# A selective state-space stage on Trainium2: two spare columns per scan row, the norm's root as a power on GpSimd, the residual added by TensorE, 14 instead of 12 products on GpSimd, and another order of all steps

## The chip, the cores and the metric

The kernel runs on one core of one Trainium2 chip. The metric is the time of one execution in microseconds of the device. Engines are named as in the profile: PE (TensorE), DVE (VectorE), ACT (ScalarE), POOL (GpSimd) and SP, whose queue only issues DMAs. Each engine works off its own queue in order, and engines wait for one another by semaphores.

## What is computed

The whole program is a small network over an image of 2 x 256 x 56 x 56: window attention, then six Mamba layers, then two token networks. The change touches only the six Mamba layers, a stage on tokens of width 256 with an inner width of 512 and 16 states per channel. For a batch row of 3136 tokens each layer computes:

```
residual = hidden + residual                  # width 256
x  = residual * rsqrt(mean(residual**2) + 1e-5) * norm_w
u, z = split(x @ in_w)                        # 512 each
u  = silu(causal_conv4(u) + cb)
dt_r, B, C = split(u @ xp_w)                  # 16, 16, 16
dt = softplus(dt_r @ dt_w + dt_b)
h_t = exp(dt_t * A) * h_(t-1) + (dt_t * u_t) * B_t    # 512 x 16 states
y_t = sum over states of h_t * C_t, plus u_t * D
hidden = (y * silu(z)) @ out_w
```

A layer norm stands in front of the first layer and one more root-mean-square norm behind the last.

## The kernel before

`mamba_phase` cuts the 3136 tokens into 7 chunks of T = 448. With 2 batch rows and 6 layers there are 84 chunks, worked through one after the other; a chunk index j runs over them. Inside a chunk the 512 x 16 states are taken in 32 **steps**, index s: 4 blocks k of 128 channels, 4 groups of states, 2 halves. One step handles two rows of T tokens on 128 partitions, side by side in one tile.

A step consists of these operations, each a small function:

- `inputs` (L809): ACT copies the state kept from the chunk before into the first column of each row of the tile `x`, and POOL multiplies `dtur` (dt times u, spread over partitions) by B (`bc`) into the other columns (L816).
- `decays` (L791): ACT computes exp(dt * A) into the PSUM tile `da`, one instruction for each of the two rows (L799). Column 0 of `dtr` holds 1e30, so that the decay there is 0 and the scan starts afresh in each row.
- `scan` (L833): one DVE instruction runs the recurrence over both rows, 2 x 449 = 898 columns. Its result goes back into `da`, or into `x` where the step is listed in `on_pool`.
- the product with C (`times_c`, L829): on DVE directly behind the scan, or, for the 12 steps of `on_pool`, later on POOL in place in `x` (`pool_product`).
- `keep` (L823): ACT copies the last column of each row into the state.
- `gather` (L840), for every second step: PE sums over states into the PSUM tile `acc`; `gate` (L857), for every eighth: DVE multiplies by silu(z).
- `fetch`: SP loads `dtr` and `dtur` for the next k from DRAM.

Beside these 32 steps the projections for the next chunk run: `u_project`, `u_convolve`, `x_project`, `dt_project` and others on PE, all through a single PSUM bank `mm`, each followed by a copy or an activation on ACT. `y_project` (L696) multiplies by `out_w`, and `y_add` (L705) adds the result to the residual on DVE. The norm takes `n_squares` (ACT square, PE mean), `n_root` (ACT, Sqrt), `n_invert` (DVE, reciprocal), `n_spread` (PE) and `n_weighted` (DVE). The tables `first` and `last` hold the same for the layer norm in front and the final norm. Tiles `x` come from a pool of 9 buffers, `da` from 3, `acc` and `mm` from one each.

The order is written out by hand: every operation gets a **place** in units of steps, a number added to the index of its step or chunk, and all are issued sorted by place. A place is thus no time; it only fixes the order of each engine's queue. Before, all steps have the same offsets:

```
put(i - 1.652, inputs, i)
put(i - 1.217, decays, i)
put(i + 0.4, scan, i)
put(i + 1.080, keep, i)
if i % ns in on_pool: put(i + 2.886, pool_product, i)
if i % 2 == 1: put(i + 3.900, gather, i)
if i % 8 == 7: put(i + 4.422, gate, i)
```

Of the kernel before, what the change touches and what calls it, by code (L numbers as in the profile page):

```python
# [453 lines left out]
def mamba_phase(ctx: ExitStack, tc: tile.TileContext, I, t1_d, t2_d):  # L454
# [9 lines left out]
    ctx.enter_context(tc.manual_schedule())  # L464
    T = MT
    cp = ctx.enter_context(tc.tile_pool(name="mb_const", bufs=1))
# [12 lines left out]
    nc.vector.memset(mean_w, 1.0 / C)  # L479
    eps = ones_column(nc, cp, 1e-5, "mb_eps")  # L480
    sum_w = cp.tile([P, HD], F32, name="sum_w")
    nc.sync.dma_start(sum_w, I["sum_w"])
# [4 lines left out]
    res = cp.tile([P, 2, S], F32, name="res")  # L487
    dtrs = [cp.tile([P, 4, T + 1], F32, name=f"dtr{n}") for n in range(2)]
    for t in dtrs:
        nc.gpsimd.memset(t[:, :, 0:1], BIG)  # L490

    r1_d = [dp.tile([P, 2, T], F32, name=f"r1_d{c}", bufs=1) for c in range(MCH)]

    def wide(t, n=2):
        return t.unsqueeze(1).to_broadcast([P, n, T])

# [112 lines left out]
    def x_keep(j):  # L609

        xd = M["xd"] = one.tile([DTR + 2 * DS, T], F32, name="xd")
        nc.scalar.copy(xd, M["mm"])  # L612
        bc_d = dp.tile([2 * DS, T], F32, name="bc_d")
        nc.sync.dma_start(bc_d, xd[DTR:, :])
        bc = QS[j + 1]["bc"] = two.tile([P, 8, T + 4], F32, name="bc")[:, :, 3 : T + 3]
        for n in range(4):
            nc.sync.dma_start(
                bc[chunk(n, HD)],
                bc_d.rearrange("(m n) t -> n m t", n=4)[n].unsqueeze(0).to_broadcast([HD, 8, T]),
            )  # L620
        QS[j + 1]["dt_d"], QS[j + 1]["dtu_d"] = {}, {}
# [41 lines left out]
    def root(key):  # L663
        rs = M[key] = one.tile([MTG, ng], F32, name="rs" + key)
        nc.scalar.activation(rs, M["mm"][:MTG, :ng], AF.Sqrt, bias=eps[:MTG])

    def invert(key):
        nc.vector.reciprocal(M[key], M[key])

# [26 lines left out]
    def y_project(j, k):  # L696

        ps = M["mm"] = mm()[:, :T]
        for d in range(NB):
            nc.tensor.matmul(  # L700
                ps, lhsT=layer_of(j - 1)["w_out"][:, d, chunk(k, P)],
                rhs=QS[j - 1]["hz"][:, d, :], start=(d == 0), stop=(d == NB - 1),
            )

    def y_add(j, k):  # L705
        rc = residual(j - 1)
        nc.vector.tensor_tensor(rc[:, k, :], rc[:, k, :], M["mm"], ALU.add)  # L707

# [58 lines left out]
    def repeat(Q, k):  # L767

        dtr = dtrs[k % 2]
        dtur = two.tile([P, 4, T + 4], F32, name="dtur")[:, :, 1 : T + 1]  # L770
        for t, src in ((dtr[:, :, 1:], Q["dt_d"]), (dtur, Q["dtu_d"])):
            for n in range(4):
                nc.sync.dma_start(t[chunk(n, HD)], src[k].rearrange("(g p) t -> p g t", p=HD))
        Q[k] = dtr, dtur
# [4 lines left out]

    on_pool = (2, 3, 5, 7, 8, 9, 10, 15, 19, 21, 22, 26)  # L780
    chunks = [(b, layer, c) for b in range(B) for layer in range(NL) for c in range(MCH)]
# [9 lines left out]
    def decays(i):  # L791
# [3 lines left out]
        da = pda.tile([P, 1024], F32, name="da")  # L795
        D[i] = da[:, : 2 * (T + 1)]
        for g in range(2):
            col = (4 * k + 2 * pr + g) * 4 + ng
            nc.scalar.activation(  # L799
                D[i][:, chunk(g, T + 1)], dtr[:, 2 * pr + g, :], AF.Exp,  # L800
                scale=L["am"][:, col : col + 1],
            )
# [6 lines left out]
    def inputs(i):  # L809

        j, s, k, ng, pr = at(i)
        Q = QS[j]
        X[i] = xp.tile([P, 2 * (T + 1)], F32, name="x")
        x = both(X[i])
# [8 lines left out]
    def keep(i):  # L823
        h = X[i] if i % ns in on_pool else D[i]
        nc.scalar.copy(states(i), both(h)[:, :, T : T + 1])  # L825

    def times_c(i, engine, h):
        j, s, k, ng, pr = at(i)
        engine.tensor_tensor(  # L829
            both(X[i])[:, :, 1:], both(h)[:, :, 1:], wide(QS[j]["bc"][:, 4 + ng, :]), ALU.mult  # L830
        )

    def scan(i):  # L833

        h = X[i] if i % ns in on_pool else D[i]
        nc.vector.tensor_tensor_scan(h, D[i], X[i], 0.0, ALU.mult, ALU.add)  # L836
        if i % ns not in on_pool:
            times_c(i, nc.vector, h)

    def gather(i):  # L840
# [9 lines left out]
        for g in range(4):  # L850
            nc.tensor.matmul(  # L851
                acc[0][chunk(g, HD), :T], lhsT=sum_w, rhs=both(X[i - 1 + g // 2])[:, g % 2, 1:],
                start=False, stop=(ng == 3), tile_position=(0, HD * g),
# [8 lines left out]

    def pool_product(i):
        times_c(i, nc.gpsimd, X[i])

# [17 lines left out]
    def load_rest(j):  # L883
# [5 lines left out]
    places = {  # L889
        (u_project, 0): 1.304, (u_keep, 0): 2.607, (z_project, 0): 3.501, (z_keep, 0): 3.952,  # L890
        (u_project, 1): 4.609, (u_keep, 1): 5.234, (y_project, 1): 6.869, (y_add, 1): 7.331,
        (y_project, 0): 7.461, (y_add, 0): 9.223, (u_convolve, 0): 10.048, (u_add, 0): 10.687,
        (u_project, 2): 10.964, (u_keep, 2): 11.995, (u_convolve, 1): 12.277, (u_add, 1): 13.134,
        (u_convolve, 2): 14.792, (u_add, 2): 15.184, (u_project, 3): 15.393, (u_keep, 3): 16.616,
        (u_convolve, 3): 17.440, (u_add, 3): 17.991, (z_project, 1): 18.040, (u_silu,): 18.479,
        (z_keep, 1): 18.732, (x_project,): 19.334, (x_keep,): 20.167, (dt_project, 2): 20.825,
        (dt_keep, 2): 21.601, (dt_project, 0): 21.808, (dt_keep, 0): 22.204,
        (dt_project, 1): 23.295, (dt_keep, 1): 23.374, (dt_project, 3): 24.269,
        (dt_keep, 3): 24.913, (dt_softplus,): 24.942, (dt_out, 0): 25.013, (dt_back,): 25.337,
        (z_project, 2): 25.840, (dt_out, 1): 26.057, (z_keep, 2): 26.747, (z_project, 3): 27.262,  # L900
        (load,): 27.272, (dt_out, 2): 27.694, (z_keep, 3): 28.791, (n_squares,): 29.547,
        (n_root,): 29.821, (n_invert,): 31.105, (n_spread,): 32.629, (n_weighted,): 32.761,
        (load_rest,): 34.587, (dt_out, 3): 36.194, (z_silu,): 38.909,
    }
    first = {
        f_load: 12.141, f_mean: 23.145, f_center: 23.266, f_squares: 23.712, s_root: 23.835,
        s_invert: 24.267, s_spread: 25.138, f_scale: 25.476,
    }
    last = {
        l_squares: 0.000, s_root: 0.000, s_invert: 1.571, s_spread: 2.712, l_weighted: 3.271,  # L910
        f_load: 5.288, l_out: 5.690,
    }
# [14 lines left out]
    for i in range(n):  # L927
        put(i - 1.652, inputs, i)
        put(i - 1.217, decays, i)
        put(i + 0.4, scan, i)  # L930
        put(i + 1.080, keep, i)
        if i % ns in on_pool:
            put(i + 2.886, pool_product, i)
        if i % 2 == 1:
            put(i + 3.900, gather, i)
        if i % 8 == 7:
            put(i + 4.422, gate, i)
        if i % 8 == 0 and i % ns < ns - 8:
            put(i + 1.264, fetch, i)
    for j in range(-2, nj + 1):  # L940
# [559 lines left out]
```

## Time and profile before

| | before |
|---|---|
| median of 3 runs | 9829.77 us (9820.45 to 9840.27) |
| profiled execution | 9833.15 us, span 9831.3 us, granted clock 0.867 |
| first and last scan start | 693.4 us and 8489.3 us |
| DVE busy in the span | 8388.8 us (85%) |
| POOL busy | 7120.1 us (72%) |
| ACT busy | 6758.1 us (69%) |
| PE busy | 7995.7 us (81%) |

The profile is one execution. Its page gives busy time and counts of each engine, the span in 40 slices, the chain that ended last, and groups of instructions by line with their mean duration and the idle time before them. Durations of neighbours on one engine overlap a little; the time that an instruction takes from its engine is read from the starts of consecutive instructions in the timeline.

### The profile page before, as it was taken

How to read it: one execution, taken by the hardware profiler on the slowest of the kernel's cores; microseconds unless marked ns; L12 is line 12 of the kernel's file. 1: busy time of each engine (PE TensorE's matmuls, PEld its weight loads, DVE VectorE, ACT ScalarE, POOL GpSimd, SP SyncE). 2: the span in 40 equal slices, each digit the busy share in tenths (PEclk: the TensorE clock that was granted, in tenths of full speed). 3: DMA queues.
4: the chain of work that ended last, by engine and by line, in shares of the span. 5: the costliest groups of instructions: out<-in, count | busy, mean ns of one | idle time of the engine just before them, and what ended most of it. 6: DMA issues, size and time to landing. Idle time of an engine off the chain costs nothing. (4 is left out here: it accounts for less than half of the span.)

```text
span 9831.3 us, 102094 instructions
## 1 busy us (share of the span) xinstructions
PE 7995.7 (81%) x31026; PEld 3378.5 (34%) x31026; DVE 8388.8 (85%) x6835; ACT 6758.1 (69%) x15177; POOL 7120.1 (72%) x4860
## 2 busy tenths in 40 slices
PE   9877777777777777777777877787777777699999
PEld 6533323322222222232222222222222223255555
DVE  3338999899999999999999999999999999685453
ACT  1127777777877878777778787787877877534443
POOL 2347888788888888888898888888889888511110
PEclk9988888788888888888888888888888888799999
DMA  2235555455555555556555555555555555301111
GB/s 81 70 100 113 115 132 120 114 132 123 128 121 128 131 114 131 127 124 142 122 127 131 122 124 128 126 121 124 133 118 123 134 121 127 104 19 34 42 41 38
DMA packets 681950, 1083.41 MB, mean 110 GB/s; under 512 B 83532, under 2 KB 673169, under 8 KB 681169
## 3 DMA queue, kind: packets, MB, share of 16 engines
q1 hardware_dynamic: 681398, 1076.90, 47.1%
q8 instruction: 243, 3.98, 0.2%
q14 instruction: 309, 2.53, 0.1%
HBM read 891.71 MB, written 184.91 MB: 110 GB/s over the span
## 5 line engine op out<-in xcount | busy, mean ns | idle before, releaser
L816 POOL TENSOR_TENSOR x<-dtur,bc 128x896 f32<-128x896 f32 x2688 | 4706.5, 1775 | 109.6 <-PE acc L851 100.0
L799 ACT ACTIVATE da<-dtr,am 128x449 f32<-128x449 f32 x5376 | 3428.5, 638 | 188.1 <-DVE x L836 95.8
L836 DVE TENSOR_TENSOR_SCAN da<-da,x 128x898 f32<-128x898 f32 x1680 | 3397.1, 2022 | 144.7 <-ACT da L799 71.3
L829 POOL TENSOR_TENSOR x<-x,bc 128x896 f32<-128x896 f32 x1008 | 1791.2, 1777 | 510.6 <-ACT state L825 509.2
L554 PE MATMUL mm<-xn,w_in 128*128 128x448 f32 x2656 | 1483.3, 691 | 710.5 <-ACT hz L595 236.1
L836 DVE TENSOR_TENSOR_SCAN x<-da,x 128x898 f32<-128x898 f32 x1008 | 2001.8, 2013 | 0.7 <-ACT da L799 0.7
L829 DVE TENSOR_TENSOR x<-da,bc 128x896 f32<-128x896 f32 x1680 | 1834.4, 1092 | 80.6 <-PE mm L572 0.9
L851 PE MATMUL acc<-x,sum_w 128*32 128x448 f32 x10752 | 1565.9, 658 | 25.2 <-POOL x L829 17.7
L572 PE MATMUL mm<-u,w_cv 128*128 128x448 f32 x2656 | 1088.5, 552 | 175.5 <-ACT u L566 158.8
L554 PEld LDWEIGHTS mm<-xn,w_in 128*128 128x128 f32 x2656 | 550.3, 230 | 1684.5 <-issue 731.5
L825 ACT COPY state<-da 128x2 f32<-128x2 f32 x1680 | 264.2, 157 | 1059.4 <-DVE x L829 1041.8
L572 PEld LDWEIGHTS mm<-u,w_cv 128*128 128x128 f32 x2656 | 476.7, 189 | 801.5 <-issue 371.8
L644 POOL TENSOR_TENSOR dtu<-dt,hz 128x448 f32<-128x448 f32 x336 | 329.7, 981 | 463.4 <-ACT state L825 413.0
L700 PE MATMUL mm<-hz,w_out 128*128 128x448 f32 x1344 | 552.0, 554 | 80.2 <-DVE res L707 47.8
L625 PE MATMUL mm<-xd,w_dt 16*128 16x448 f32 x664 | 454.4, 772 | 190.7 <-ACT xd L612 111.1
L851 PEld LDWEIGHTS acc<-x,sum_w 128*32 128x32 f32 x10752 | 229.7, 117 | 1002.7 <-issue 792.2
L815 ACT COPY x<-state 128x2 f32<-128x2 f32 x2688 | 521.7, 194 | 0.0
L1348 DVE TENSOR_TENSOR hid<-hid,cb 128x784 f32<-128x784 f32 x128 | 135.2, 1057 | 423.8 <-ACT hid L1345 400.4
L799 ACT ACT_TABLE_LOAD x346 | 443.9, 1283 | 7.0 <-DMA dtr<-dt_d 1.0
L658 PE MATMUL mm<-mb_mean_w,sq 128*112 128x1 f32 x1744 | 259.5, 279 | 231.0 <-ACT sq L654 230.2
L846 PE MATMUL acc<-hz,w_sk 128*128 128x448 f32 x672 | 369.4, 635 | 63.1 <-DVE hz L861 61.8
L700 PEld LDWEIGHTS mm<-hz,w_out 128*128 128x128 f32 x1344 | 242.5, 190 | 403.7 <-issue 191.2
(217 smaller groups left out, 8949.1 us busy)
## 6 DMA issues: line engine op xcount, KB each, us to landing
dtr<-dt_d SPq DMA_DIRECT2D x1344, 224.0 KB
dtur<-dtu_d SPq DMA_DIRECT2D x1344, 224.0 KB
bc<-bc_d SPq DMA_DIRECT2D x336, 448.0 KB
dt_d<-dt SPq DMA_DIRECT2D x336, 224.0 KB
dtu_d<-dtu SPq DMA_DIRECT2D x336, 224.0 KB
cb<-comb_d SPq DMA_DIRECT2D x128, 196.0 KB
t<-t_d SPq DMA_DIRECT2D x28, 448.0 KB
w_in<-in_in_w SPq DMA_DIRECT2D x12, 1024.0 KB
```

What stands on the lines that cost most here:

```text
L554: nc.tensor.matmul(ps, lhsT=layer_of(j + 1)["w_in"][:, k, chunk(at, P)], rhs=Q["xn"][:, k, :], start=(k == 0), stop=(k == 1),)
L572: nc.tensor.matmul(ps, lhsT=layer_of(j + 1)["w_cv"][:, 4 * d + k, :], rhs=M["u", d][:, k : k + T], start=(k == 0), stop=(k == 3),)
L625: nc.tensor.matmul(ps, lhsT=layer_of(j + 1)["w_dt"][:, chunk(d, P)], rhs=M["xd"][:DTR, :], start=True, stop=True,)
L644: nc.gpsimd.tensor_tensor(dtu, dt[:, d, :], hz(j)[:, d, :], ALU.mult)
L700: nc.tensor.matmul(ps, lhsT=layer_of(j - 1)["w_out"][:, d, chunk(k, P)], rhs=QS[j - 1]["hz"][:, d, :], start=(d == 0), stop=(d == NB - 1),)
L799: nc.scalar.activation(D[i][:, chunk(g, T + 1)], dtr[:, 2 * pr + g, :], AF.Exp, scale=L["am"][:, col : col + 1],)
L815: nc.scalar.copy(x[:, :, 0:1], states(i))
L816: nc.gpsimd.tensor_tensor(x[:, :, 1:], Q[k][1][:, 2 * pr : 2 * pr + 2, :], wide(Q["bc"][:, ng, :]), ALU.mult)
L829: engine.tensor_tensor(both(X[i])[:, :, 1:], both(h)[:, :, 1:], wide(QS[j]["bc"][:, 4 + ng, :]), ALU.mult)
L836: nc.vector.tensor_tensor_scan(h, D[i], X[i], 0.0, ALU.mult, ALU.add)
L846: nc.tensor.matmul(acc[0][:, :T], lhsT=L["w_sk"][:, k, :], rhs=Q["hz"][:, k, :], start=True, stop=False,)
L851: nc.tensor.matmul(acc[0][chunk(g, HD), :T], lhsT=sum_w, rhs=both(X[i - 1 + g // 2])[:, g % 2, 1:], start=False, stop=(ng == 3), tile_posi ...
```

## The change

- Rows get two trailing columns: R = T + 3 = 451, a scan has 902 columns. `dtr`, `dtur` and `bc` hold zeros there (set once; `dtur` and `bc` become two fixed tiles each), so the decay is 1, the input 0, and the last column repeats the last state. `keep` reads the last column; the product with C covers only the T real ones. `inputs` on POOL is 2 x 450 wide.
- `root` uses ACT's Identity (adds 1e-5) instead of Sqrt; `invert` raises to the power -0.5 on POOL instead of a reciprocal on DVE.
- `y_project` gets a fifth matmul, identity times residual, in the same PSUM group; `y_keep` on ACT copies the sum into the residual instead of DVE's addition.
- `on_pool` lists 14 other steps. The product is an operation with a place of its own, on DVE too.
- `inputs`, `decays`, `product`, `keep`, `gather` and `gate` have places of their own for each step, and all places of the projections and norms are new.

```diff
+    half = ones_column(nc, cp, -0.5, "half")
...
-    dtrs = [cp.tile([P, 4, T + 1], F32, name=f"dtr{n}") for n in range(2)]
+    dtrs = [cp.tile([P, 4, R], F32, name=f"dtr{n}") for n in range(2)]
+    dturs = [cp.tile([P, 4, T + 4], F32, name=f"dtur{n}")[:, :, 1:R] for n in range(2)]
+    bcs = [cp.tile([P, 8, T + 4], F32, name=f"bc{n}")[:, :, 2:] for n in range(2)]
...
-        nc.scalar.activation(rs, M["mm"][:MTG, :ng], AF.Sqrt, bias=eps[:MTG])
+        nc.scalar.activation(rs, M["mm"][:MTG, :ng], AF.Identity, bias=eps[:MTG])
...
-        nc.vector.reciprocal(M[key], M[key])
+        nc.gpsimd.tensor_tensor(
+            M[key], M[key], half[:MTG].to_broadcast([MTG, ng]), ALU.pow
+        )
...
+        nc.tensor.matmul(ps, lhsT=ident, rhs=residual(j - 1)[:, k, :], start=False, stop=True)
...
-        nc.vector.tensor_tensor(rc[:, k, :], rc[:, k, :], M["mm"], ALU.add)
+    def y_keep(j, k):
+        nc.scalar.copy(residual(j - 1)[:, k, :], M["mm"])
...
-    on_pool = (2, 3, 5, 7, 8, 9, 10, 15, 19, 21, 22, 26)
+    on_pool = (0, 1, 4, 10, 11, 13, 14, 16, 19, 21, 26, 27, 28, 29)
...
-        nc.scalar.copy(states(i), both(h)[:, :, T : T + 1])
+        nc.scalar.copy(states(i), both(h)[:, :, R - 1 :])
...
+    def product(i):
+        if i % ns in on_pool:
+            times_c(i, nc.gpsimd, X[i])
+        else:
+            times_c(i, nc.vector, D[i])
...
+        (y_project, 1): 1.94872, (y_keep, 1): 2.18416, (y_project, 0): 4.51846,
+        (y_keep, 0): 4.93098, (u_convolve, 0): 5.73491, (u_add, 0): 6.45942,
...
+        (z_keep, 3): 25.37533, (n_squares,): 25.49637, (dt_out, 1): 25.68262, (dt_back,): 26.15343,
+        (n_root,): 26.78672, (n_invert,): 27.20493, (load,): 27.30912, (n_spread,): 27.87557,
+        (n_weighted,): 28.16785, (z_silu,): 28.29135, (load_rest,): 34.90000,
...
+        product: (
+            2.0693, 1.5054, 1.4500, 0.4361, 1.4010, 2.0711, 1.4010, 0.4933, 1.0351, 0.9825, 2.2000,
+            0.4701, 1.0348, 0.4500, 0.4010, 0.4010, 2.6797, 0.4825, 1.4502, 1.9106, 0.5150, 1.5798,
+            1.4066, 1.4024, 0.7375, 0.4500, 1.4500, 1.5733, 1.9449, 1.4053, 1.6036, 0.9000,
+        ),
```

## The prediction

> **What bounds the kernel now.** I read the page's busy times and its slices first, then the stage table, then the groups of the steady part, the waits of DVE and POOL, and last the two timelines.
>
> ```profile
> PE 7995.7 (81%) x31026; PEld 3378.5 (34%) x31026; DVE 8388.8 (85%) x6835; ACT 6758.1 (69%) x15177; POOL 7120.1 (72%) x4860
> ...
> DVE  3338999899999999999999999999999999685453
> ```
>
> The slices show DVE at 9 in nearly all of the Mamba stage (from about 690 to 8490 us), so the 85% is an average over stages. The stage table, for a steady 1000 us (columns: bounds, length, then busy us and count of PE, PEld, DVE, ACT, POOL; clock, DMA share, GB/s):
>
> ```profile
> 2400.00:3400.00 1000.00, 789.87 (x2817) 284.89 (x2816) 970.99 (x672) 797.82 (x1869) 881.69 (x535) 0.85 0.56 126
> ```
>
> DVE is 97% busy, POOL 88%, ACT 80%, PE 79%: DVE is the bound. From 2400 to 7400 us the groups that matter (count, then busy us and mean ns, then idle time before them and what ended it) are:
>
> ```profile
> L836 DVE TENSOR_TENSOR_SCAN da<-da,x 128x898 f32<-128x898 f32 x1093 | 2210.1, 2022 | 95.8 <-ACT state L825 48.5 <-ACT da L799 47.3
> L836 DVE TENSOR_TENSOR_SCAN x<-da,x 128x898 f32<-128x898 f32 x654 | 1298.7, 2013 | 0.0
> L829 DVE TENSOR_TENSOR x<-da,bc 128x896 f32<-128x896 f32 x1093 | 1193.5, 1092 | 53.4 <-PE mm L572 0.5
> L829 POOL TENSOR_TENSOR x<-x,bc 128x896 f32<-128x896 f32 x654 | 1162.0, 1777 | 338.1 <-ACT state L825 337.3
> ...
> L644 POOL TENSOR_TENSOR dtu<-dt,hz 128x448 f32<-128x448 f32 x220 | 215.8, 981 | 208.4 <-ACT state L825 208.4
> ...
> L707 DVE TENSOR_TENSOR res<-res,mm 128x448 f32<-128x448 f32 x108 | 65.1, 603 | 0.0
> ```
>
> 1747 scans in 5000 us are 54.6 chunks, so a chunk takes **91.6 us**. DVE's real waits are few: 95.8 us in front of scans and 20.4 in front of `xn`, 2.1 us per chunk. The 53.4 before products is no wait for another engine: 49 ns each, a product reading what the scan just wrote. What an instruction takes from DVE is read from starts:
>
> ```profile
> 4999.01 2.02 DVE L836 TENSOR_TENSOR_SCAN da<-da,x 128x898 f32<-128x898 f32 x1
> 5001.07 1.09 DVE L829 TENSOR_TENSOR x<-da,bc 128x896 f32<-128x896 f32 x1
> 5002.08 2.02 DVE L836 TENSOR_TENSOR_SCAN da<-da,x 128x898 f32<-128x898 f32 x1
> ...
> 5031.39 3.94 DVE L836 TENSOR_TENSOR_SCAN x<-da,x 128x898 f32<-128x898 f32 x2
> 5035.24 0.59 DVE L861 TENSOR_TENSOR hz<-hz,acc 128x448 f32<-128x448 f32 x1
> ```
>
> A scan with its product takes 2.06 + 1.01 = 3.07 us; a scan alone 3.85 / 2 = 1.93. In the same way `gate` takes 0.53, `y_add` 0.52, the pair of `xn` 1.18, the reciprocal 0.09. Check: 20 x 3.07 + 12 x 1.93 + 4 x 0.53 + 2 x 0.52 + 1.14 norms x (1.18 + 0.09) = 89.2, plus 2.1 waits = 91.3, against 91.6 measured.
>
> **The change on DVE, per chunk.** Two products leave: 2 x (3.07 - 1.93) = -2.28. `y_add` leaves: 2 x 0.52 = -1.04. The reciprocal leaves: -0.10. The product now has a place: of the 18 left on DVE, 7 have 1.4 or more and so stand behind the next scan, which should take away the read-after-write gap and lets neighbours overlap; a detached pair should take 1.93 + 1.01 = 2.94 to 2.98 instead of 3.07: 7 x 0.11 = -0.77. Four more columns at (2.022 us / 898) = 2.25 ns: 32 x 0.009 = +0.29. Sum **-3.9**: DVE needs 89.2 - 3.9 = 85.3 us per chunk before waits.
>
> **POOL, per chunk.** Seven `inputs` in a row take 12.10 us in the timeline, 1.73 each; a product takes the same, a `dtu` 0.94. Before: 44 x 1.73 + 4 x 0.94 + 0.4 (final norm, layer loads) = 80.3, and the table's POOL busy over five such stretches, 4385.2 / 54.6, gives 80.3. The change adds 2 x 1.73 = 3.46, and 32 x 4 columns x 2 ns = 0.25: 84.0, plus the power. No row shows a power. Its nearest rows are POOL's smallest operations, 0.20 us for 128x2 and 0.43 for 128x64, so it can't be below 0.2; from above nothing bounds it, and I keep 5 us as the far end. I take 1.0 (0.2 fixed and 4 columns at a hundred times a product's 2 ns, an estimate). At 1.14 norms a chunk: POOL 85.1.
>
> [...] The rows here give 1777 against 1092 ns, 1.63. [...] The measured row decides: 85.1.
>
> **What POOL no longer waits for.** Before, the in-place product on POOL overwrote the column that `keep` reads, so it waited for ACT: 337.3 us, 6.2 per chunk. With the trailing column it waits for the scan alone. This was POOL's slack, so the gain is only that the added 4.8 us of POOL work find room.
>
> **ACT.** Each norm's Sqrt costs a table load and a reload for Exp, 1283 ns each: 2 x 1.14 x 1.28 = -2.9. Two `y_keep` of 0.52 us, about 0.43 each with overlap: +0.9. Columns +0.1. [...] The timeline shows the exponentials 0.02 us behind a load, so I take -2.9. ACT falls from 3975.7 / 54.6 = 72.8 to 70.9, 81% of the new period. It isn't the bound; it matters where a `decays` stands behind something late. The new waits: `y_keep` waits for five matmuls, and the next exponentials stand behind it. For k = 1 the scan that needs them is 2.1 steps on. For k = 0 the chain is `y_project` 4.52, `y_keep` 4.93, `decays` of step 6 at 5.33, its scan at 6.4: 1.07 steps, some 2.9 us, less 1.3 for the exponentials and about 1 for the rest of the matmuls. That is covered by half a microsecond; uncovered it costs at most 1 us per chunk.
>
> **PE** gets two matmuls of 353.6 / 864 = 0.41 us: +0.8 on 72.1 per chunk, hidden. Its queue waits at `n_spread` for the power, which may stand behind a running POOL product (up to 1.7 us), and DVE waits behind it at `n_weighted`; before, that wait cost 20.4 us in 5000, 0.4 per chunk.
>
> **DMA and buffers.** SP issues a `fetch` once the last readers of its tiles are done, not at its place; by the places of these readers the first `inputs` of the next k stand 4.9 steps (13 us) or more behind that, and POOL waited 0.2 us in 5000 for such a load before. In SP's queue the second `dt_out` now stands ahead of `dt_back`, the next chunk's first loads: they wait for one more `dtu` (0.94) and two issues (0.34 each in SP's timeline), 1.6 us, and their first reader, `decays` at 30.70, is 4.5 steps behind `dt_back` at 26.15, so 12 us cover it; without that cover it would be 1.6 us per chunk. The third `dt_out` moves from 27.7 to 37.4, behind the layer's weight loads; its data are wanted only for k = 2. An `x` buffer comes free with its `gather`: by places the ninth `inputs` after stood 2.45 steps or more behind it, now 0.22 to 0.38 at four points, so there is little reserve. POOL waited 61.8 us there before, 1.1 per chunk; I let it grow to 2.
>
> **The sum.** DVE 85.3, POOL 85.1 plus its waits for `softplus` and buffers, about 2. Two engines feeding each other at 97% each lose a little; I put DVE's waits at 2.7 instead of 2.1. Period 88.0, a gain of 3.6 x 84 chunks = 302 us. In the first chunks DVE waited 47 us for the layer norm's root (`rss` from ACT), a wait that goes to POOL; half of it counts, -20, the bounds being 0 and -47. The final chain gets slightly longer, +3. 9833 - 319 = 9514 for the profiled execution; the median of the runs stood 3 us below it: **9510**.
>
> **Rivals.**
> - *POOL becomes the bound.* At 85.1 with 3.8 us of waits at `dtu` (208.4 / 54.6, as now) and 1.1 at buffers the period is 90.0: 84 x 1.6 = 134, less 20: 9680. For it: `dtu` still waits for `softplus`, and POOL's reserve falls from 11 us to 3. Against it: `dt_out` stands 0.8 steps behind `softplus` now, 0.07 before. Chance 0.22.
> - *The power is dear, and the kernel slower.* POOL's 84.0 reaches 91.6 when 1.14 powers fill 7.6 us, at 6.7 us each, or at 3.3 with POOL's present waits at `dtu` beside it. At 7 us with these waits: 84.0 + 8.0 + 3.8 = 95.8, +350: 10180; a narrow miss at 5 us gives 93.5, +160: 9990. For it: no row shows a function of this kind on POOL. Against it: only four columns. Chance 0.09.
> - *DVE hardly waits.* With 0.9 us of waits, 86.2: 84 x 5.4 = 454 + 20: 9360. For it: ACT stood idle 666 us at `keep`, waiting for DVE products, and many `keep` now stand ahead of them. Against it: some exponentials stand only 0.24 to 0.3 steps ahead of their scan. Chance 0.09.
>
> **How the numbers follow.** The forecast case (period 87 to 89, 9420 to 9600) has 0.60. To leave out at most 0.2 the range must reach POOL-bound cases on top and part of the fast ones below: 9400 to 9740. Some 0.2% (20 us) is what a measurement can tell. Slower: the dear power and a tenth of the POOL-bound cases, 0.11; within 0.2%: 0.03; faster 0.86.
>
> **What will show it.** Scans per 1000 us rise from 350 to about 364. DVE's `res` and reciprocal rows vanish, products number 1512, and pairs with a scan between lose their gap. POOL's busy share reaches 96% or more; its wait at products names DVE. Sqrt table loads are gone, and 109 of 346 reloads. A power row over 4 us, or a DVE wait for POOL at scans above 3 us per chunk, proves the forecast wrong.

## The result and the profile after

| | before | after |
|---|---|---|
| median of 6 runs | 9829.77 us (9819.1 to 9845.21) | 9796.74 us (9786.09 to 9801.04) |
| profiled execution | 9833.15 us, span 9831.3 us | 9795.2 us, span 9793.4 us |
| granted clock | 0.867 | 0.873 |

The ratio is 0.9965, with an interval of 0.9952 to 0.9977: 33 us faster, where 320 had been forecast. The sign is right, the size is not, and the time lies above the range on record (9400 to 9740).

The page of the changed kernel, busy times and the slices of DVE and POOL:

```profile
PE 8175.8 (83%) x31362; PEld 3469.1 (35%) x31362; DVE 8083.2 (83%) x6388; ACT 6611.1 (68%) x15130; POOL 7545.9 (77%) x5146
...
DVE  3339999999999999998999999999999999685453
...
POOL 1339999899999999999999999999999999511110
```

DVE works 306 us less than before and POOL 426 us more, as planned. But the slices can't say more than 9; the stage table of the steady 5000 us can (columns: bounds, length, then busy us and count of PE, PEld, DVE, ACT, POOL; clock, DMA share, GB/s):

```profile
2400.00:7400.00 5000.00, 4049.34 (x14337) 1499.31 (x14336) 4628.68 (x3066) 3887.52 (x9224) 4648.82 (x2819) 0.85 0.56 126
```

DVE and POOL are both 93% busy, and neither is full. The groups of the same stretch (count, then busy us and mean ns, then idle time before them and what ended it):

```profile
L823 POOL TENSOR_TENSOR x<-dtur,bc 128x900 f32<-128x900 f32 x1746 | 3060.5, 1781 | 172.1 <-PE acc L857 168.4
...
L844 DVE TENSOR_TENSOR_SCAN da<-da,x 128x902 f32<-128x902 f32 x982 | 1981.9, 2030 | 263.7 <-POOL x L823 134.6 <-ACT state L832 57.3 <-ACT da L806 53.8
L844 DVE TENSOR_TENSOR_SCAN x<-da,x 128x902 f32<-128x902 f32 x762 | 1525.1, 2023 | 31.0 <-ACT da L806 26.2 <-ACT x L822 1.9 <-POOL x L823 1.0
L836 POOL TENSOR_TENSOR x<-x,bc 128x896 f32<-128x896 f32 x763 | 1345.6, 1773 | 28.7 <-DVE x L844 26.0 <-PE acc L857 0.8
L836 DVE TENSOR_TENSOR x<-da,bc 128x896 f32<-128x896 f32 x982 | 1046.1, 1083 | 49.0 <-ACT state L832 25.8
...
L822 ACT COPY x<-state 128x2 f32<-128x2 f32 x1745 | 302.8, 189 | 189.7 <-PE acc L857 184.7 <-POOL dtu L650 3.4
L650 POOL TENSOR_TENSOR dtu<-dt,hz 128x448 f32<-128x448 f32 x218 | 211.0, 978 | 63.0 <-ACT state L832 63.0
```

982 + 762 = 1744 scans are 54.5 chunks, 91.7 us each, against 91.6 before: in the steady part nothing was gained. DVE's busy time per chunk did fall, from 4828.94 / 54.6 = 88.5 us to 84.9, but its waits for others rose from 2.1 us to 6.4: 5.4 in front of scans, 0.5 in front of products (25.8 us for ACT), 0.5 in front of `xn`. Two rows are new: scans wait for POOL's `inputs` (134.6), and ACT's copy into `x` (L822) waits 184.7 us for a `gather` on PE. Before, that copy waited for nothing:

```profile
L815 ACT COPY x<-state 128x2 f32<-128x2 f32 x1746 | 338.8, 194 | 0.0
```

The 33 us come from the first 18 chunks, which had been slower than the later ones: up to 2400 us a chunk takes (2400 - 704.3) x 32 / 579 scans = 93.7 us, before (2400 - 693.4) x 32 / 563 = 97.0. That is 60 us, less 11 because the first scan starts at 704.3 instead of 693.4, less 66 chunks x 0.15 us: 39, against a difference of 38 in the spans.

**Where the wait arises.** One spot comes back from chunk to chunk, and its row (POOL x L823) makes 134.6 / 54.5 = 2.5 us of each. The timeline (start, duration, then the operation, its count, and in brackets the idle time before it) shows TensorE's queue between 5033 and 5046 us:

```profile
5034.43 1.01 PE L631 MATMUL mm<-xd,w_dt 16*128 16x448 f32 x2 [1.68 <-ACT xd L618]
5036.35 1.85 PE L631 MATMUL mm<-xd,w_dt 16*128 16x448 f32 x2 [0.90 <-ACT dt L637]
5038.93 1.85 PE L631 MATMUL mm<-xd,w_dt 16*128 16x448 f32 x2 [0.72 <-ACT dt L637]
5040.71 1.86 PE L852 MATMUL acc<-hz,w_sk 128*128 128x448 f32 x2
5042.50 1.72 PE L857 MATMUL acc<-x,sum_w 128*32 128x448 f32 x8
```

The last line is the `gather` of steps 16 and 17. In the same stretch POOL, then ACT, then DVE:

```profile
5033.53 1.77 POOL L836 TENSOR_TENSOR x<-x,bc 128x896 f32<-128x896 f32 x1
...
5044.40 1.78 POOL L823 TENSOR_TENSOR x<-dtur,bc 128x900 f32<-128x900 f32 x1 [3.89 <-PE acc L857]
```

```profile
5044.31 0.20 ACT L822 COPY x<-state 128x2 f32<-128x2 f32 x1 [2.40 <-PE acc L857]
5044.50 2.55 ACT L806 ACTIVATE da<-dtr,am 128x451 f32<-128x451 f32 x4
```

```profile
5042.34 2.02 DVE L844 TENSOR_TENSOR_SCAN da<-da,x 128x902 f32<-128x902 f32 x1
5047.14 2.04 DVE L844 TENSOR_TENSOR_SCAN da<-da,x 128x902 f32<-128x902 f32 x1 [2.78 <-POOL x L823]
```

Read it backwards. The scan of step 23 waits 2.78 us. The profile names POOL's `inputs`, but those of step 23 had been over since 5037.0, and the ones that run until 5046.18 are step 24's; what ended last is the pair of exponentials for step 23 on ACT, the second half of the four that end at 5047.05. They stand in ACT's queue behind the copy for step 24, and that copy waits for one of the 9 buffers of `x`, the one that the `gather` of step 16 gives back. The product of step 16 was ready at 5035.30. Its `gather` starts at 5042.50, because by its place (17 + 3.3422 = 20.34) it stands in PE's queue behind `dt_project` 0, 2 and 3 (19.35, 20.04, 20.28), which share the one bank `mm`, so that each waits for ACT to read the one before. ACT is needed for the projections, PE for ACT's buffer, and DVE waits for both. The 7.20 us from product to `gather` are the longest case of this stretch; over its 54 chunks, counted in the trace, the median is 5.7 us and the shortest 4.0.

The granted clock of TensorE makes this chain longer. The stage table of the same few microseconds (the clock is the third number from the end):

```profile
5034.00:5036.00 2.00, 1.01 (x2) 0.29 (x2) 2.00 (x2) 1.97 (x6) 2.00 (x2) 1.00 0.12 29
5036.00:5038.00 2.00, 1.65 (x2) 0.49 (x2) 2.00 (x3) 0.57 (x3) 2.00 (x2) 0.55 0.24 85
5038.00:5046.00 8.00, 7.28 (x15) 1.70 (x14) 6.32 (x4) 5.26 (x11) 4.11 (x3) 0.50 1.06 206
```

It falls from 1.00 to 0.50, and two matmuls of `dt_project` take 1.85 us instead of 1.01. For the three groups between 5036.35 and the `gather` that is 3 x 0.84 = 2.5 of the 7.2 us, an estimate; the rest is the standing behind them.

### The profile page after: what moved, and what is told of

Its sections match the earlier page's. It is cut to its first block, busy times and chain, and to the rows that moved or that the text cites. A ratio compares the mean times of both kernels' runs of the same rounds, so it can differ in the third digit from the quotient of the medians.

```text
span 9793.4 us, 102137 instructions
## 1 busy us (share of the span) xinstructions
PE 8175.8 (83%) x31362; PEld 3469.1 (35%) x31362; DVE 8083.2 (83%) x6388; ACT 6611.1 (68%) x15130; POOL 7545.9 (77%) x5146
## 5 line engine op out<-in xcount | busy, mean ns | idle before, releaser
L823 POOL TENSOR_TENSOR x<-dtur,bc 128x900 f32<-128x900 f32 x2688 | 4712.4, 1781 | 285.4 <-PE acc L857 272.0
L806 ACT ACTIVATE da<-dtr,am 128x451 f32<-128x451 f32 x5376 | 3400.6, 638 | 367.0 <-DVE x L844 220.5
L844 DVE TENSOR_TENSOR_SCAN da<-da,x 128x902 f32<-128x902 f32 x1512 | 3050.7, 2030 | 358.5 <-POOL x L823 176.5
L844 DVE TENSOR_TENSOR_SCAN x<-da,x 128x902 f32<-128x902 f32 x1176 | 2353.9, 2022 | 51.8 <-ACT da L806 34.7
L836 POOL TENSOR_TENSOR x<-x,bc 128x896 f32<-128x896 f32 x1176 | 2074.0, 1773 | 63.0 <-DVE x L844 59.1
L560 PE MATMUL mm<-xn,w_in 128*128 128x448 f32 x2652 | 1344.7, 635 | 494.8 <-ACT hz L590 244.9
L836 DVE TENSOR_TENSOR x<-da,bc 128x896 f32<-128x896 f32 x1512 | 1610.3, 1083 | 83.8 <-ACT state L832 49.4
L578 PE MATMUL mm<-u,w_cv 128*128 128x448 f32 x2656 | 1186.0, 593 | 203.3 <-ACT res L715 184.5
L578 PEld LDWEIGHTS mm<-u,w_cv 128*128 128x128 f32 x2656 | 515.8, 204 | 866.4 <-issue 426.2
L631 PE MATMUL mm<-xd,w_dt 16*128 16x448 f32 x664 | 482.8, 817 | 232.8 <-ACT dt L637 134.6
L822 ACT COPY x<-state 128x2 f32<-128x2 f32 x2688 | 466.4, 189 | 287.2 <-PE acc L857 280.5
L852 PE MATMUL acc<-hz,w_sk 128*128 128x448 f32 x672 | 469.4, 791 | 41.9 <-DVE hz L867 41.8
L610 PE MATMUL mm<-hz,w_xp 128*48 128x448 f32 x664 | 339.6, 666 | 140.0 <-ACT state L832 140.0
L590 ACT ACTIVATE hz<-mm,vec 128x448 f32<-128x448 f32 x332 | 207.0, 624 | 277.8 <-PE mm L578 277.8
```

The source lines that it names most:

```text
L560: nc.tensor.matmul(ps, lhsT=layer_of(j + 1)["w_in"][:, k, chunk(at, P)], rhs=Q["xn"][:, k, :], start=(k == 0), stop=(k == 1),)
L578: nc.tensor.matmul(ps, lhsT=layer_of(j + 1)["w_cv"][:, 4 * d + k, :], rhs=M["u", d][:, k : k + T], start=(k == 0), stop=(k == 3),)
L631: nc.tensor.matmul(ps, lhsT=layer_of(j + 1)["w_dt"][:, chunk(d, P)], rhs=M["xd"][:DTR, :], start=True, stop=True,)
L806: nc.scalar.activation(D[i][:, chunk(g, R)], dtr[:, 2 * pr + g, :], AF.Exp, scale=L["am"][:, col : col + 1],)
L822: nc.scalar.copy(x[:, :, 0:1], states(i))
L823: nc.gpsimd.tensor_tensor(x[:, :, 1:], Q[k][1][:, 2 * pr : 2 * pr + 2, :], wide(Q["bc"][:, ng, :]), ALU.mult)
```

## The experiments

All numbers in the table are of the same steady 5000 us, except the medians. The ratio is against the kernel before, run beside it on the same chip. "Work" is DVE's busy time per chunk, "idle" is the chunk's period less this; idle includes the short gaps between an instruction and the next that reads its result (1.0 us per chunk before, 0.4 after).

| kernel | median us | ratio (interval) | period | DVE work | DVE idle |
|---|---|---|---|---|---|
| before | 9829.77 | 1 | 91.6 | 88.5 | 3.1 |
| after | 9796.74 | 0.9965 (0.9952 to 0.9977) | 91.7 | 84.9 | 6.8 |
| e1: after, one gather earlier | 9647.08 | 0.9807 (0.979 to 0.9824) | 89.9 | 84.9 | 5.0 |
| e2: after, keep 15 and decays 18 earlier | 9875.96 | 1.0041 (1.0028 to 1.0055) | 92.6 | 84.9 | 7.7 |
| e3: both | 9793.12 | 0.9956 (0.9939 to 0.9972) | 91.6 | 85.1 | 6.6 |
| e4: after, 11 buffers for x | 9677.3 | 0.9841 (0.9821 to 0.9861) | 90.1 | 84.8 | 5.3 |
| e5: all parts, old order, 12 products | 9902.91 | 1.0064 (1.0047 to 1.0081) | 92.6 | 87.7 | 4.9 |
| e6: all parts, old order, 14 products | 9675.67 | 0.9834 (0.982 to 0.9849) | 90.0 | 85.3 | 4.7 |
| e7: e1 and e4 together | 9655.26 | 0.9812 (0.9796 to 0.9827) | 90.2 | 85.0 | 5.2 |
| e8: after, silu and softplus left out | 9581.68 | 0.9737 (0.9722 to 0.9751) | 88.7 | 84.5 | 4.3 |
| e9: e8 with e1's gather | 9676.0 | 0.9845 (0.983 to 0.986) | 90.3 | 84.5 | 5.8 |
| e10: e5, residual on DVE | 9881.85 | 1.0052 (1.0035 to 1.0069) | 92.5 | 88.7 | 3.8 |
| e11: e1, residual on DVE | 9865.81 | 1.0039 (1.0024 to 1.0054) | 92.7 | 86.2 | 6.5 |
| e12: e6, residual on DVE | 9621.69 | 0.9788 (0.9774 to 0.9803) | 89.2 | 86.3 | 2.8 |
| e13: before, 14 products | 9630.52 | 0.9796 (0.9782 to 0.9811) | 89.5 | 86.2 | 3.3 |
| e14: before, power | 9845.09 | 1.0006 (0.9994 to 1.0017) | 92.2 | 88.4 | 3.8 |
| e15: before, two columns | 9878.7 | 1.0047 (1.0032 to 1.0062) | 92.3 | 88.7 | 3.6 |
| e16: before, 14 products and power | 9619.23 | 0.9784 (0.977 to 0.9799) | 89.2 | 86.1 | 3.1 |

### The late gather, the silu block, and buffers (e1 to e4, e7)

My theory after reading the trace was that two places cause the wait: the `gather` of steps 16 and 17, and the stretch of ACT with `u_silu`, behind which the exponentials of step 18 stand. The rival was a general one: DVE and POOL feed each other so closely that work taken from one shows up as a wait in the other wherever places are moved.

e1 moves one place, 17 + 3.3422 to 17 + 3.0000, so that the `gather` stands behind `dt_project` 0 alone:

```diff
-            5.4231, 5.3545, 4.1209, 3.9096, 3.9826, 4.2190, 4.0799, 2.3619, 3.3422, 5.9161, 3.9778,
+            5.4231, 5.3545, 4.1209, 3.9096, 3.9826, 4.2190, 4.0799, 2.3619, 3.0000, 5.9161, 3.9778,
```

> The changed kernel with one place moved: the gather of steps 16 and 17 stands ahead of the projection of dt for k = 2 in TensorE's queue instead of behind three of them (its place 20.34 becomes 20.00). Theory 1 (a queue head): in every chunk this gather is ready at about 5035 us but runs at 5042 to 5044, behind projections that wait for ScalarE; the x buffer that it frees is late, ScalarE's state copy stands waiting 2.4 us for that buffer in front of two exponentials, and VectorE waits 2.5 to 3.0 us at the scan of step 23. Then the wait goes and the time falls by 84 x about 2.3 = 190, to 9600. Theory 2 (coupling): with VectorE and GpSimd each needing 85 of 91.7 us the loss sits in the coupling through few buffers, the wait only turns up elsewhere, and the time stays within 30 us of 9797.

Measured 9647.08 us, 150 us below the changed kernel. In e1's timeline of PE the `gather` follows directly behind the first projection:

```profile
3135.08 1.01 PE L631 MATMUL mm<-xd,w_dt 16*128 16x448 f32 x2 [0.62 <-ACT xd L618]
3136.03 1.02 PE L852 MATMUL acc<-hz,w_sk 128*128 128x448 f32 x2
3136.98 0.96 PE L857 MATMUL acc<-x,sum_w 128*32 128x448 f32 x8
3137.87 1.01 PE L631 MATMUL mm<-xd,w_dt 16*128 16x448 f32 x2
```

and in its groups the wait for POOL's `inputs` has left the scans that write `da`, and two thirds of ACT's wait for buffers is gone:

```profile
L844 DVE TENSOR_TENSOR_SCAN da<-da,x 128x902 f32<-128x902 f32 x1000 | 2018.3, 2030 | 158.5 <-ACT da L806 57.1 <-ACT state L832 56.4 <-issue 40.0
...
L822 ACT COPY x<-state 128x2 f32<-128x2 f32 x1775 | 308.7, 189 | 65.0 <-PE acc L857 62.2 <-POOL x L823 1.2
```

DVE's idle time falls by 1.8 us per chunk, and 84 x 1.8 = 151 is the whole gain. This one place cost 150 us; the forecast of 190 was somewhat high. The edit moved two things at once, though: the `gather` now starts 0.06 us behind its product (median of the stretch), and in the lines above it takes 0.96 us instead of 1.72, with `dt_project` beside it at 1.01 instead of 1.85. What a late and slow `gather` costs when nobody needs its buffer is seen in e4.

e2 moves `keep` of step 15 and `decays` of step 18 ahead of the silu:

```diff
@@ decays, step 18
-            -0.0209, -0.7899, -0.3644, -1.0665, -0.0863, -0.8027, -0.8400, -2.6685, 0.1130,
+            -0.0209, -0.7899, -0.3644, -1.0665, -0.0863, -0.8027, -0.8400, -2.6685, -1.6800,
@@ keep, step 15
-            1.8006, 1.9964, 2.2501, 1.1706, 2.1249, 2.5011, 1.1766, 1.2541, 0.7378, 0.9654, 2.4106,
+            1.8006, 1.9964, 2.2501, 1.1706, 1.3000, 2.5011, 1.1766, 1.2541, 0.7378, 0.9654, 2.4106,
```

> The changed kernel with two places moved: keep of step 15 and decays of step 18 stand ahead of the copy of z block 1 and the silu of u (with its two table loads) in ScalarE's queue. Theory 1 (a queue head): VectorE's wait of 0.9 to 2.5 us per chunk at the scan of step 18, whose exponentials stand behind 4.5 us of silu and table loads, goes; 84 x about 1.2 = 100 us less, 9700. Theory 2 (coupling): the wait turns up at the next scans, within 30 us of 9797.

Measured 9875.96, 79 us slower than the changed kernel. The changed kernel's wait of 2.49 us at scan 18 is gone, but the product of that step waits now. The group of DVE's products in e2:

```profile
L836 DVE TENSOR_TENSOR x<-da,bc 128x896 f32<-128x896 f32 x972 | 1036.0, 1083 | 133.9 <-ACT state L832 111.2
```

Its wait for `keep` is 111.2 us instead of 25.8, most of it at step 18. Product and `keep` of such a step both read the tile `da`, and in these traces the later of the two in the order waits for the other (before, ACT waited 666.3 us at `keep` for DVE's products). The `keep` of step 18 kept its place in ACT's queue, behind the silu and the copy that follows `x_project`; the scan came earlier, so its product now stands waiting for it. The theory holds for the gather and falls for this place.

> Both edits of the two runs before in one kernel. Theory 1: the gains add, about 290 us, 9510. Theory 2: no more than 50 us.

e3 (both edits) measured 9793.12, far from the 9510 of a sum of gains: +146 on e1. The two are not independent, but the second is a loss with either.

e4 leaves all places and gives `x` 11 buffers instead of 9. The room comes from a constant matrix of a later stage, which is replaced by one of its columns:

```diff
-    xp = ctx.enter_context(tc.tile_pool(name="mb_x", bufs=9))
+    xp = ctx.enter_context(tc.tile_pool(name="mb_x", bufs=11))
...
-    mean_w = cp.tile([P, P], F32, name="mb_mean_w")
+    mean_w = cp.tile([P, 1], F32, name="mb_mean_w")
...
-                ps, lhsT=mean_w, rhs=A["t1"][:, k, :], start=(k == 0), stop=(k == 1)
+                ps, lhsT=mean_w.to_broadcast([P, P]), rhs=A["t1"][:, k, :], start=(k == 0), stop=(k == 1)
```

> The changed kernel with 11 buffers for x instead of 9 (room is made by a one-column mean weight that is broadcast as the stationary operand). Theory 1: the wait for the x buffer behind the late gather goes, on GpSimd (3.1 us per chunk) and on ScalarE (3.4 us per chunk), without the order being touched; about 190 us less, 9600, like the moved gather. Theory 2 (coupling through few buffers): more buffers should help even more than one moved gather, 250 us or more. Theory 3 (TensorE's load itself or the granted clock is the cause): no change.

Measured 9677.3: 119 us below the changed kernel, with ACT's wait for buffers down from 184.7 us to nothing. The `gather` is as late as before (median 5.9 us) and the matmuls ahead of it are as slow, 855 ns on average for `dt_project` and 796 for the one into `acc` (L852), against 836 and 788 in the changed kernel and 733 and 681 in e1; that nobody waits for its buffer is enough. So the slow matmuls alone don't cost DVE the time: here they mattered only through the buffer. e7 has both:

> The changed kernel with the moved gather and 11 x buffers together. Theory 1 (both take away the same wait): little more than either, 9620 to 9650. If the two took away different waits: 9797 - 150 - 120 = 9530.

Measured 9655.26, no better than e1. So the two edits take away the same wait, the chain from the late `gather` over the `x` buffer and ACT's queue to DVE, and it is worth 119 to 150 us.

### The order or the parts (e5, e6)

e5 has all parts of the change with the order of before and its 12 products; e6 adds two products:

```diff
-    on_pool = (0, 1, 4, 10, 11, 13, 14, 16, 19, 21, 26, 27, 28, 29)
+    on_pool = (2, 3, 5, 7, 8, 9, 10, 13, 15, 19, 21, 22, 26, 29)
...
+        put(i - 1.652, inputs, i)
+        put(i - 1.217, decays, i)
...
+        if i % ns not in on_pool:
+            put(i + 0.4, product, i)
+        put(i + 1.080, keep, i)
+        if i % ns in on_pool:
+            put(i + 2.886, product, i)
+        if i % 2 == 1:
+            put(i + 3.900, gather, i)
```

with the tables of places for the projections and norms of before; e5's list is the 12 steps of before.

> The changed kernel with the order of before: uniform places for all steps, the places of before for projections and norms, the 12 products of before on GpSimd. What is left of the change are the two columns, the power on GpSimd and the residual on TensorE. Theory 1 (the parts are good, the new order loses): VectorE's work falls by 1.04 + 0.10 - 0.29 = 0.85 us per chunk with the waits of before, 9830 - 70 = 9760. Theory 2 (coupling): same, as GpSimd has slack here; this run serves as the base of the next.

> The run before with two more steps, 13 and 29, on GpSimd, 14 as in the change, still in the order of before. Theory 1 (it is the new order that loses): VectorE needs 2.3 us less per chunk, GpSimd has the room: 9760 - 190 = 9570. Theory 2 (two engines at 85 us each lose their gain in coupling, whatever the order): no better than 9740.

Measured 9902.91 and 9675.67, 143 and 106 us above what the first theory gave. So columns, power and the residual on TensorE together make the kernel before 0.64% slower (e5), though they take 0.8 us of work per chunk from DVE; two more products on POOL then gain 227 us (e6). And the same parts in the old order beat the changed kernel by 121 us: the new order, as it stands, is a loss. (The 14 steps on POOL are other ones in the two orders; which of the two, list or order, costs more was not separated.)

### ACT's functions (e8, e9)

e8 replaces Silu and Softplus by Identity and Square. It leaves out these functions and with them six table loads of 1.28 us per chunk: the steady 5000 us have 326 of them in the changed kernel and none in e8.

```diff
-        nc.scalar.activation(hz(j)[:, :NB, :], hz(j)[:, :NB, :], AF.Silu)
+        nc.scalar.activation(hz(j)[:, :NB, :], hz(j)[:, :NB, :], AF.Identity)
...
-        nc.scalar.activation(M["dt"], M["dt"], AF.Softplus)
+        nc.scalar.activation(M["dt"], M["dt"], AF.Square)
```

> The changed kernel with Identity in place of Silu and Square in place of Softplus (in the Mamba stage only): these functions are left out, and with them six table loads per chunk, 7.7 us of ScalarE's 71; the order and all else stay. Theory 3 (ScalarE's blocks of 4.3 us, two loads and a function, are what VectorE waits for at the scans): VectorE's waits for exponentials and keeps, about 3 us per chunk, go, and the projections behind them come sooner; 9797 - 250 = 9550 or less. Theory 1 (gather behind the projections): only that part goes which ScalarE's delay makes, 100 us or less.

> The changed kernel with the moved gather, and with Identity and Square in place of Silu and Softplus (left out, with their six table loads per chunk). If the gain that was forecast went into these two waits (the gather behind the projections, and ScalarE's function blocks), VectorE is left with about 1 us of waits per chunk: period 86.5, 9450. If the coupling of two engines at 85 us each costs more than that whatever the queues, it stays above 9550.

e8 measured 9581.68: 7.7 us per chunk less work on ACT, which isn't the bound, brings 215 us, 2.6 per chunk, a little less than the 250 of the third theory. e9, e8 with the moved `gather`, missed clearly: 9676.0 instead of the further gain that I expected. PE's loads of the summing weights in e9 show a new wait:

```profile
L857 PEld LDWEIGHTS acc<-x,sum_w 128*32 128x32 f32 x7080 | 179.3, 116 | 763.1 <-issue 394.1 <-POOL x L836 204.3 <-DVE x L836 109.5
```

With a quicker ACT the moved `gather` reaches the head of PE's queue before POOL has finished its product, and waits there, 204.3 us (none among its three main causes in e1); the projections stand behind it, and ACT's activation behind `dt_project` waits 267.3 us for them, against 116.6 in e1. Of the 204.3 us, 145.2 stand before this one `gather`, counted in the trace. It is the first fault turned round. That it makes the whole loss of 94 us against e8 was not shown. In these runs the worth of a place depended on the speeds around it, and gains of such moves could not be added.

### The residual (e10 to e12)

Each puts the addition of the residual back on DVE, in e5, e1 and e6:

```diff
-        nc.tensor.matmul(ps, lhsT=ident, rhs=residual(j - 1)[:, k, :], start=False, stop=True)
...
-        nc.scalar.copy(residual(j - 1)[:, k, :], M["mm"])
+        rc = residual(j - 1)
+        nc.vector.tensor_tensor(rc[:, k, :], rc[:, k, :], M["mm"], ALU.add)
```

> The order of before, 12 products on GpSimd, two columns and the power on GpSimd, but the residual added on VectorE again. Theory 4 (each piece that leaves VectorE beside a block of ScalarE is lost, and the copy that ScalarE gets lengthens the block): with y_keep VectorE's waits rose from 2.1 to 3.9 us per chunk for 1.0 us of work saved; without it they fall back to 2.5 or so and the time is 9800 to 9850, better than the 9903 with the residual on TensorE. If the columns or the power are what made that kernel slower than before, it stays at 9900 or more.

> The changed kernel with the moved gather and the residual added on VectorE again. Theory 4: VectorE's work rises by 1.0 us per chunk, ScalarE's waits behind y_project go; in the new order nothing waited visibly at y_keep, so it should be slower than 9647, by up to 80, 9650 to 9730. If y_keep costs as in the old order, it is faster, 9600.

> The order of before with 14 products on GpSimd (9676), the residual on VectorE again. Theory 4: the 1.1 us wait per chunk at the block that holds y_keep goes against 1.0 us of work: 9640 to 9690. If y_keep is innocent: 9676 + 85 = 9760.

In the old order with 14 products the residual on TensorE and ACT is a loss, 9675.67 against 9621.69, although it takes 1.0 us of work per chunk from DVE. With 12 products it gains nothing: 9902.91 against 9881.85 were measured on different chips, and the intervals of their ratios overlap. (9800 to 9850 had been expected for e10.) In e5 the scans that write `x` wait 67.5 us for ACT's exponentials, in e10 4.7. ACT's timeline in e5 shows one such place, where `y_keep` (L715) and a table load stand ahead of them:

```profile
3016.39 1.70 ACT L604 ACTIVATE hz<-hz 128x1792 f32<-128x1792 f32 x1
3017.99 0.15 ACT L832 COPY state<-da 128x2 f32<-128x2 f32 x1
3018.03 0.54 ACT L715 COPY res<-mm 128x448 f32<-128x448 f32 x1
3018.45 0.21 ACT L822 COPY x<-state 128x2 f32<-128x2 f32 x1
3018.68 1.28 ACT L806 ACT_TABLE_LOAD   x1
3019.98 1.31 ACT L806 ACTIVATE da<-dtr,am 128x451 f32<-128x451 f32 x2
```

In the new order it is the other way round: e11 is 219 us slower than e1, far outside the 9600 to 9730 expected; 1.3 us of it per chunk are work, the rest a wait. The convolution's matmuls (L578) wait 243.6 us for DVE's addition to free `mm`, where the changed kernel waited 124.7 for ACT's copy. The new places fit a copy on ACT, and not an addition in DVE's queue.

e12 decides the rival. The stage table of e12:

```profile
2400.00:7400.00 5000.00, 3977.40 (x14518) 1443.71 (x14516) 4840.80 (x3265) 3915.11 (x9373) 4768.76 (x2897) 0.89 0.57 129
```

DVE is 97% busy and POOL 95% in the same 5000 us. Two engines that feed each other can both be nearly full, so coupling by itself doesn't explain the changed kernel's 93 and 93.

### Each part alone on the kernel before (e13 to e16)

```diff
@@ e13
-    on_pool = (2, 3, 5, 7, 8, 9, 10, 15, 19, 21, 22, 26)
+    on_pool = (2, 3, 5, 7, 8, 9, 10, 13, 15, 19, 21, 22, 26, 29)
@@ e14
-        nc.scalar.activation(rs, M["mm"][:MTG, :ng], AF.Sqrt, bias=eps[:MTG])
+        nc.scalar.activation(rs, M["mm"][:MTG, :ng], AF.Identity, bias=eps[:MTG])
...
-        nc.vector.reciprocal(M[key], M[key])
+        nc.gpsimd.tensor_tensor(
+            M[key], M[key], half[:MTG].to_broadcast([MTG, ng]), ALU.pow
+        )
@@ e15
-    T = MT
+    T, R = MT, MT + 3
...
-            both(X[i])[:, :, 1:], both(h)[:, :, 1:], wide(QS[j]["bc"][:, 4 + ng, :]), ALU.mult
+            both(X[i])[:, :, 1 : T + 1], both(h)[:, :, 1 : T + 1],
+            wide(QS[j]["bc"][:, 4 + ng, :T]), ALU.mult,
```

> The kernel before with steps 13 and 29 added to the products on GpSimd, nothing else. By the sum VectorE needs 2.3 us less per chunk: 9830 - 190 = 9640 if GpSimd's waits for keep (6.2 us per chunk) fit into its slack, which falls from 11 to 8 us. If the trailing columns are what makes room for these products, GpSimd can't follow and it stays above 9750.

> The kernel before with the power on GpSimd in place of Sqrt and reciprocal, nothing else. ScalarE has two table loads less per norm, VectorE 0.1 us: 9810 to 9830. If the power, waiting in GpSimd's queue, is what cost 50 us in the run with columns and power, 9870 or more.

> The kernel before with the two trailing columns alone. By the sum 0.29 us per chunk more on VectorE, 25 us: 9855. If the columns are what cost 50 us or more (GpSimd, which no longer waits for keep, now runs ahead until it waits for x buffers, and the state copies wait with it), 9880 or more.

> The kernel before with 14 products on GpSimd and the power, without columns and with the residual on VectorE. If both parts do what the sum says, 9640 - 10; if the columns are worth having once GpSimd is full, slower than the 9622 of the same kernel with columns.

- **14 products alone: 9630.52**, a gain of 202 us (against 9832.51 beside it), where the sum from the trace says 2 x 1.14 x 84 = 192. The stage table of e13 has DVE at 4814.46 us and POOL at 4678.57: POOL did 782 products in this stretch instead of 654, out of its slack.
- **The power alone: 9845.09**, ratio 1.0006 (0.9994 to 1.0017): nothing. ACT works 2.8 us less per chunk, but DVE's idle time doesn't fall (3.1 before, 3.8 here).
- **The columns alone: 9878.7**, 46 us slower. Of these, 32 x 0.009 us x 84 = 24 are the width, an estimate from the 2.25 ns per column of a scan. POOL's product no longer waits for `keep` (337.3 us before), but the group of `inputs` in e15 shows where POOL waits instead:

```profile
L821 POOL TENSOR_TENSOR x<-dtur,bc 128x900 f32<-128x900 f32 x1731 | 3051.1, 1785 | 277.3 <-PE acc L855 277.3
...
L842 DVE TENSOR_TENSOR_SCAN da<-da,x 128x902 f32<-128x902 f32 x1084 | 2201.2, 2031 | 121.1 <-ACT state L830 74.4 <-ACT da L804 46.6
```

277.3 us for buffers of `x`, against 61.8 before. POOL wasn't the bound, so a wait taken from it turned into a wait for the next thing. The second line has the other loss: scans wait 74.4 us for ACT, against 48.5.

- **14 products and the power: 9619.23**, 178 us below the changed kernel and level with e12 (9621.69), the two fastest versions that compute all. Since e12 has the columns in addition, they cost nothing that can be told once POOL has 14 products, against 46 us with 12. Its list differs from the kernel of before in the two added steps and the power only. DVE works 86.1 us per chunk, 1.2 more than in the changed kernel, and idles 3.1 instead of 6.8.

## Why the prediction was wrong

**The work was forecast well.** The sum gave 85.3 us per chunk for DVE; its busy time is 84.9. POOL: 85.1 against 4648.82 / 54.5 = 85.3. ACT: 70.9 against 3887.52 / 54.5 = 71.3. The unknown price of the power, taken as 1.0 us, is in the group of the changed kernel

```profile
L674 POOL TENSOR_TENSOR rsn<-rsn,half 112x4 f32<-112x4 f32 x54 | 54.6, 1012 | 75.0 <-ACT x L822 75.0
```

1012 ns, so the dear power is out. A product on POOL took 1773 ns against 1083 on DVE, near the 1777 and 1092 taken from the rows of before, and e13 got its full gain from two of them. POOL's products no longer wait for `keep` (337.3 us before), only 26.0 us for scans. The Sqrt loads went (62 in the steady 5000 us before, none after), and the reloads for Exp fell from 218 to 163. In the first 18 chunks most of the gain came, 60 us of 18 x 3.6 + 20 = 85. The right sign comes from there and from nowhere else; in the steady part, on which the argument rests, nothing was gained.

**The step that failed** is "I put DVE's waits at 2.7 instead of 2.1". They are 6.4. The 3.7 us between are, over 84 chunks, 311 us, against a gap of 287 between 9797 and 9510. I had treated waits as a small rest that grows a little. The `x` buffers were looked at, but by the wrong measure: "now 0.22 to 0.38 at four points, so there is little reserve. POOL waited 61.8 us there before, 1.1 per chunk; I let it grow to 2." The pair that cost the time, the `gather` of steps 16 and 17 at 20.34 and the `inputs` of step 24 at 21.33, is 0.99 steps apart; it is not one of the four points, and nine pairs are closer. A distance in places takes the `gather` to run at its place; it stands behind three projections that each wait for ACT to free `mm`, and ran 4.0 to 7.2 us after its data were there. And the buffer has a second waiter: ACT's copy (L822), which the prediction never priced, waits 3.4 us per chunk, with the exponentials of the next scans queued behind it. POOL's wait grew to 168.4 / 54.5 = 3.1, less than the 6.4 us per chunk that POOL was idle.

The sign named for a wrong forecast, a wait of DVE for POOL above 3 us per chunk, didn't show: it is 2.5, and even these are named after POOL while ACT ended last. PE, put at 72.9 us per chunk and hidden, took 4049.34 / 54.5 = 74.3; its slow stretch at half clock is part of the chain, and was not thought of.

**The statement "POOL becomes the bound"** (9680) did not happen: POOL is idle 6.4 us per chunk, and its wait at `dtu` fell to 63.0 us instead of staying at 208.4. The rivals all asked which engine fills up. None said that no engine fills up because the queues hold one another, and that is the case that came.

**What the 33 us are made of.** Five of the runs make a path from the kernel before to the changed one, with one thing altered at each step (medians of different chips, on which the kernel before took 9829.77 to 9839.72, so to some 10 us):

| step | from | to | us |
|---|---|---|---|
| two more products on POOL (e13) | 9832.51 | 9630.52 | -202 |
| the power (e16) | 9630.52 | 9619.23 | -11 |
| the columns (e12) | 9619.23 | 9621.69 | +2 |
| the residual on TensorE (e6) | 9621.69 | 9675.67 | +54 |
| the new order, with its own list of 14 steps (the changed kernel) | 9675.67 | 9796.74 | +121 |

The prices hold for this path only. With 12 products the columns cost 46 (e15) and the power gives nothing (e14); in the new order the residual on TensorE is a gain (e1 against e11). Of the order's loss the late `gather` explains all and more: without it (e1) the new order is some 29 us ahead of the old one with the same parts, and still 28 behind e16.

**What stays open.** e1 still idles 5.0 us per chunk, where e12 and e16 idle 2.8 and 3.1 in the old order. The waits are spread over ACT's exponentials and `keep`; e8 shows that ACT's functions have a part in them and e9 that this part can't be added to the rest. Which place causes which was not settled. The granted clock of the whole stretch doesn't order the runs: it is 0.87 in e1 (89.9 us per chunk) and in e2 (92.6). Why the clock falls in the chain was not tried. Nor was it tried why scans wait more for ACT in e15, or why the first scan starts 11 us later.

## What to carry to other kernels

A sum of work per engine gives a floor; here, whether it was reached was decided at the heads of the queues. For every operation that hands back a buffer, look at what stands ahead of it in its queue and what those wait for, then at everyone who waits for that buffer and at what stands behind them. Where parts can be had singly, measure them singly: here one part (two products moved) carried the gain, and the residual and the new order, meant to take work and waits off the bound engine, gave most of it back.

Two more buffers took ACT's wait for them from 184.7 us to nothing and brought 119 us (e4). An earlier `gather` took it to 62.2 us with no more memory, and brought 150 (e1): before adding buffers, ask why the one that is missing comes back late.

## What the runs showed of the hardware

- TensorE's matmuls slowed down in this chain: the granted clock fell from 1.00 to 0.50 at 5036.2, two matmuls of `dt_project` went from 1.01 to 1.85 us, and the `gather` took 1.72, against 0.96 in e1, where it follows directly behind other work. PE's pauses in front of the three `dt_project` lines shown are 1.68, 0.90 and 0.72 us long. What sets the clock was not shown.
- A power on GpSimd over 112x4 elements takes 1012 ns, five times the 0.21 us of its operations over 128x2, and less than a product over 128x896, 1773 ns.
- The operation named as the end of a wait need not be its cause: for scan 23 the trace names POOL's `inputs`, while ACT's exponentials ended last, at 5047.05.
